# P x V in two groups per quad of heads instead of three, and two fillers at other slots

## The chip, the cores and the metric

The kernel runs on one core of a Trainium2 chip, as one program. The metric is the device time of one execution in microseconds; a kernel's time is the median of its runs. A profile is one further execution, recorded by the hardware profiler. TensorE (PE) multiplies matrices and writes PSUM; PEld is its weight load; VectorE (DVE), ScalarE (ACT) and GpSimd (POOL) do the rest; SyncE (SP) issues most DMAs.

## What is computed

One decoder layer in float32 over 16 sequences of 512 tokens with 256 features: causal attention with 16 heads of 16 features, and a feed-forward part whose hidden layer (1024) passes through butterfly stages before and after a Gelu. Cut to what matters:

```
q = x@wq + x@Aq@Bq*4;  k = x@wk;  v = x@wv + x@Av@Bv*4        # heads of 16
q, k = rope(q), rope(k)
scores = q@k.T / sqrt(16);  scores = where(causal, -1e9, scores)
out = softmax(scores) @ v                                     # "P x V"
x = layernorm(x + out@wo)
h = butterfly_up(x@W_exp + b_exp);  h = gelu(h + up_bias)
x = layernorm(x + butterfly_down(h)@W_con + b_con + down_bias)
```

The butterflies are folded into the two matrices once, at the kernel's beginning, so each sequence has a dense product into 1024 hidden units and one back.

## The kernel before, in words

A sequence is a batch `b`. Its 16 heads are worked through in four *quads* of four heads. The scores of a quad are made twice: once as queries by keys, from which VectorE takes the largest of each row (`largest`, L407), and three quads later, with these largest values put into the operands, as keys by queries, which ScalarE turns into exponentials (`weights`, L453) and which then multiply V (`weigh`, L504). Only the lower triangle is made, in four column blocks of a quad: block 0 has 512 columns, block 1 has 384, block 2 has 256, block 3 has 128.

The whole order is written out by hand. The main loop (L823) goes through *slots* `s`; a quad has five slots, `u` = 0 to 4, and a batch has 20. A batch's 20 slots are counted here as slots 0 to 19 of the batch whose row maxima are made in them; u=4 is at slots 4, 9, 14 and 19, and u=0 of the next quad at 5, 10, 15 and 0. In slots 15 to 319 of the run, both kinds of scores are made in each slot: `largest` for the quad of slot `s`, `weights` for the quad of slot `s - 15`. In the first 15 slots there is `largest` alone, in the last 15 (from 320) `weights` alone.

In each slot the loop does, in this order:

1. It takes two PSUM tiles, `pb` and `pa`, of two banks each; both pools have a single buffer. In slots u=0 to 3 `pb` receives the scores of `weights` and `pa` those of `largest`. In u=0 and u=1 that is block 0 of one pair of heads each, in u=2 and u=3 blocks 1 and 3 of one pair each. In u=4 it is block 2 of all four heads, so that each of `pb` and `pa` holds half of both kinds. The matmuls of the two kinds are issued in turn, two of the one and two of the other (four and four in u=4).
2. For `weights`: ScalarE's exponential from PSUM into the tile `pT` (L487) and POOL's causal mask on the diagonal (L491). For `largest`: VectorE's reduction with the mask added (L427), one per block and head.
3. P x V of those groups of blocks whose exponentials were made in an earlier slot (`weigh`, from the queue `due`). A quad's groups are `GROUPS`: group 0 is block 0, group 1 is blocks 1 and 3, group 2 is block 2. For every block and head there is one matmul into a quarter of the partitions of `po`; four heads fill its 128 partitions. A float32 matmul appears as two in the profile. When group 2 is done, ScalarE copies `po` to `oT` (L529).
4. The fillers: all other work, from the tables `others` and `holes`. The numbers in `add(s + ..., ...)` are the slots.

The tiles `pT` come from a pool with three buffers (L66), one per group; `po` has one.

Which group is put on the queue, and at which slot it is taken off (the entry has to be of an earlier slot):

```
if kinds[0][0] is weights and (u % 2 if len(kinds) == 2 and u < 4 else True):
    due.append((s, (*kinds[0][1], u // 2)))
...
while due and due[0][0] < (s if m < B * per else s - 1):
    weigh(*due.popleft()[1])
```

So with both kinds of scores group 0 is appended at u=1 and taken at u=2, group 1 appended at u=3 and taken at u=4, and group 2 appended at u=4 and taken at u=0 of the next quad.

The fillers that stand around the boundary of two quads, per batch, in the middle of the run:

| slot | u | P x V | fillers |
|---|---|---|---|
| 4 | 4 | group 1 | two hidden chunks (`hidden`, L631) |
| 5 | 0 | group 2 | two hidden chunks |
| 9 | 4 | group 1 | half a contraction (`contract`, L658), with add and statistics on VectorE |
| 10 | 0 | group 2 | half a contraction |
| 14 | 4 | group 1 | `project_v` of the third token block (L385), copied to `vaug` by ScalarE (L392) |
| 15 | 0 | group 2 | second half of the third contraction, with add and statistics |
| 19 | 4 | group 1 | two output projections (`project_out`, L561), each with add and statistics |
| 0 | 0 | group 2 | half a contraction |

`project_v(b, t)` makes V of token block `t` for batch `b`; V has two buffers, `vaugs[b % 2]`. In the first two and the last two batches of the run some of these fillers are elsewhere or missing; in the first two, tasks that fold the butterflies (`fold_tasks`) stand among them. The fillers that belong to a contraction take a bank of the pool `ps_w` (three banks) from the first half to VectorE's add behind the second.

Of the kernel before, what the change touches and what calls it, by code (L numbers as in the profile page):

```python
# [33 lines left out]
def decoder_layer(  # L34
# [19 lines left out]
    B, T, D = x.shape  # L54
# [449 lines left out]
    def weigh(b, c, par, group):  # L504
        pT = state.pop(("pT", b, c, par, group))
        if group == 0:
            state["po"] = ps_pv.tile([P, T], F32, tag="pv", name=f"po_{b}_{c}_{par}")
        po = state["po"]
        at = 0
        for k in GROUPS[group]:  # L510
            n = width(k)
            for g in range(NG):
                h = 2 * NG * c + 2 * g + par
                nc.tensor.matmul(  # L514
                    po[HG * g : HG * (g + 1), k * P : T],
                    vaugs[b % 2][:, k, h, :],
                    pT[:, g, at : at + n],
                    start=(k == 0),
                    stop=(group == 2),
                )  # L520
            at += n
        if group == 2:
            normalize_heads(b, c, par, po)
# [122 lines left out]
    def gelus(b, count=NHC):  # L646
        h = state["h", b]
        for hc in range(count):
            nc.scalar.activation(  # L649
                h[:, hc, :], h[:, hc, :], AF.Gelu, bias=hbias[:, hc : hc + 1]  # L650
            )
# [40 lines left out]
    def add(s, f, *args):  # L692
        others[s].append(lambda: f(*args))

    def start_projection(b, side, c):
        state["pr", b, side, c] = project(b, side, c)
# [16 lines left out]
    for b in range(B):  # L713
        s = b * per
        if b > 0:

            at = {1: (-16, -11, -13, -9), B - 1: (-4, 7, 7, 11)}.get(b, (-4, -3, 14, 11))
            for t in range(NT):
                add(s + at[t], project_v, b, t)
        if b + 1 < B:  # L720

            add(s - head * (b == 0), load_xT, b + 1)
            at = {0: (2, 5, 7, 10), 1: (3, 6, 8, 11)}.get(b, (7, 7, 7, 7))
            for i, (c, side) in enumerate(chains):
                holes.setdefault(s + at[i], []).append(
                    lambda b=b, side=side, c=c: start_projection(b + 1, side, c)
                )
                for step in range(3):
                    add(s + max(at[0] + 1 + 3 * i, at[i] + 1) + step, turn, b + 1, side, c, step)
                for step in range(1 + side):  # L730
                    add(s + max(at[0] + 1 + 3 * i, at[i] + 1) + 4 + step, part, b + 1, side, c, step)
        add(s + 5, load_x, b)
        add(s + 11, place_largest, b, 0)
        add(s + 21, place_largest, b, 1)
        for n in range(NQ):
            at = s + behind + PER_QUAD * n + 6 + (b + 1 == B)
            if at < end:
                add(at, turn_back, b, n // 2, n % 2)
        if b + 1 < B:
            for t in range(NT):  # L740
                add(s + (37, 37, 37, 38)[t], turn_heads, b, t)
                add(s + (38, 38, 39, 39)[t], project_out, b, t)
            add(s + 39, spread, 1, b)
            add(s + 40, offset, 1, b)
            add(s + 41, centre, 1, b)
            for c in range(NC):
                add(s + 42, turn_x1, b, c)
        if b + 2 < B:
            for hc in range(NHC):
                add(s + 43 + hc // 2, hidden, b, hc)  # L750
            holes.setdefault(s + 47, []).insert(0, lambda b=b: gelus(b))
            for t in range(NT):
                for half in range(2):
                    at = (8, 9, 10, 12, 13, 15, 20, 21)[2 * t + half]
                    add(s + 40 + at, contract, b, t, half)
            add(s + 61, spread, 2, b)
            add(s + 62, offset, 2, b)
            add(s + 62, centre, 2, b)
            add(s + 62, store, b)
# [50 lines left out]
    due = deque()  # L810

    def quad_of(s):
        n, u = divmod(s, PER_QUAD)
        return (n // NQ, n % NQ // 2, n % 2), u

    def place(blocks, ps, at=0):
        placed = []
        for block, pair in blocks:
            placed.append((block, pair, ps, at))
            at += width(block)  # L820
        return placed

    for s in range(-head, last):  # L823
        m, e = s, s - behind
        kinds = [
            (fn, *quad_of(n))
            for fn, n in ((weights, e), (largest, m))
            if 0 <= n < B * per
        ]
        parts = []  # L830
        step = 2
        if kinds and not (len(kinds) == 1 and kinds[0][2] % 2):
            u = kinds[0][2]
            pair0 = ps_b.tile([P, 2, T], F32, tag="b", name=f"pb_{s}")
            pair1 = ps_a.tile([P, 2, T], F32, tag="a", name=f"pa_{s}")
            if len(kinds) == 1:
                fn, quad, u = kinds[0]
                for r, ps in enumerate((pair0, pair1)):
                    parts.append(fn(*quad, place([(k, r) for k in GROUPS[u // 2]], ps)))
            elif u == PER_QUAD - 1:  # L840
                step = 4
                for i, (fn, quad, _) in enumerate(kinds):
                    parts.append(
                        fn(*quad, [(2, r, ps, i * 2 * P) for r, ps in enumerate((pair0, pair1))])
                    )
            else:
                for i, (fn, quad, _) in enumerate(kinds):
                    blocks = [(k, (r + i) % 2) for k, r in SLOTS[u]]
                    parts.append(fn(*quad, place(blocks, (pair0, pair1)[i])))
            if kinds[0][0] is weights and (u % 2 if len(kinds) == 2 and u < 4 else True):  # L850
                due.append((s, (*kinds[0][1], u // 2)))
        for i in range(0, max([len(p[0]) for p in parts], default=0), step):
            for p in parts:
                for f in p[0][i : i + step]:
                    f()
        for p in parts:
            p[1]()
        while due and due[0][0] < (s if m < B * per else s - 1):
            weigh(*due.popleft()[1])
        for f in others[s]:  # L860
            f()
        for f in holes.get(s, ()):
            f()
        to = 0 if s < 2 else tasks_at.get(s, len(fold))
        while given < min(to, len(fold)):
            while ahead < min(given + 3, len(fold)):
                fold[ahead][0]()
                ahead += 1
            fold[given][1]()
            given += 1  # L870
# [108 lines left out]
```

## Time and profile before

| | us |
|---|---|
| median of three runs | 1411.76 |
| lowest and highest run | 1406.98 and 1413.27 |
| the profiled execution, device time | 1415.53 |
| its span, first to last instruction | 1413.8 |
| granted TensorE clock, mean | 0.991 of full |
| TensorE matmuls | 9208 |
| bytes read from and written to HBM | 22.88 MB, 8.39 MB |

The span is what the profile's times are shares of. An engine's busy time is the time in which at least one of its instructions was under way. In a group's line, the numbers behind the bar are busy time and mean duration in ns, then the idle time of the engine just before them and what ended it. In a timeline, each line is a run of equal instructions in order of time: start, how long it lasted, engine, source line, operation, output<-inputs, shapes, and how many; a bracket at the end gives the idle time before it and the instruction that ended it. Ends of matmuls are modelled, so distances between starts are safer than durations. The batches in the middle repeat each other: in the two stretches 600.00 to 683.33 and 683.33 to 766.66 TensorE is busy for 82.84 us each, with 569 matmuls each, VectorE for 50.31 and 50.30.

### The profile page before, as it was taken

How to read it: one execution, taken by the hardware profiler on the slowest of the kernel's cores; microseconds unless marked ns; L12 is line 12 of the kernel's file. 1: busy time of each engine (PE TensorE's matmuls, PEld its weight loads, DVE VectorE, ACT ScalarE, POOL GpSimd, SP SyncE). 2: the span in 40 equal slices, each digit the busy share in tenths (PEclk: the TensorE clock that was granted, in tenths of full speed). 3: DMA queues.
4: the chain of work that ended last, by engine and by line, in shares of the span. 5: the costliest groups of instructions: out<-in, count | busy, mean ns of one | idle time of the engine just before them, and what ended most of it. 6: DMA issues, size and time to landing. Idle time of an engine off the chain costs nothing.

```text
span 1413.8 us, 24605 instructions
## 1 busy us (share of the span) xinstructions
PE 1379.7 (98%) x9208; PEld 758.6 (54%) x9208; DVE 828.0 (59%) x2846; ACT 720.1 (51%) x1120; POOL 511.0 (36%) x779
## 2 busy tenths in 40 slices
PE   8899999999999999999999999999999999998998
PEld 4454546465564645555464555545455564644565
DVE  5766656556575655657465565746556574664422
ACT  2665455544555454555445455544545555445553
POOL 3534225253342425334252433514244252521311
PEclk9998999999999999999999999999999999999999
DMA  5310000100010010001101100010011001000000
GB/s 180 114 31 16 32 31 16 61 17 32 31 47 30 17 53 24 32 31 32 46 17 42 36 32 31 23 55 16 32 46 32 31 17 60 3 31 2 16 1 30
DMA packets 36472, 50.43 MB, mean 36 GB/s; under 512 B 3704, under 2 KB 23160, under 8 KB 36352
## 3 DMA queue, kind: packets, MB, share of 16 engines
q1 hardware_dynamic: 32464, 43.30, 8.8%
q10 hardware_dynamic: 3888, 5.55, 1.3%
q8 instruction: 73, 1.20, 0.3%
q14 instruction: 47, 0.39, 0.1%
HBM read 22.88 MB, written 8.39 MB: 22 GB/s over the span
## 4 chain that ended last, share of the span: by engine, by line
PE 94%; ACT 2%; DVE 2%; issue 1%; DMA 0%; POOLq 0%; POOL 0%; DVEq 0%; ACTq 0%
PE pb L470 20%; PE py L658 17%; PE ph L631 16%; PE po L514 11%; PE pqk L339 8%; PE pwo L561 4%; PE pvv L385 4%; PE pa L418 3%; PE pto L536 2%; PE pb L418 2%; DVE junk L427 1%; PE ptm L443 1%; PE pt L614 1%; PE ptc L552 1%; PE pd L269 1%; PE pa L470 1%
## 5 line engine op out<-in xcount | busy, mean ns | idle before, releaser
L427 DVE CUSTOM_DVE_ANT_0 junk<-pa,causal 128x384 bf16<-128x384 f32 (+2 forms) x878 | 439.3, 500 | 240.9 <-PE pa L418 209.5
L487 ACT ACTIVATE pT<-pb 128x1024 f32<-128x1024 f32 (+1 forms) x314 | 293.7, 935 | 365.4 <-PE pa L418 266.6
L491 POOL TENSOR_SCALAR_AFFINE_SELECT pT<-pT 128x256 f32<-128x256 f32 x512 | 202.5, 408 | 755.6 <-ACT pT L487 751.3
L470 PE MATMUL pb<-qz,kz 17*128 17x512 f32 (+2 forms) x1756 | 330.0, 475 | 10.7 <-ACT pT L487 9.9
L418 PE MATMUL pa<-kz,qz 32*128 32x384 f32 (+3 forms) x1756 | 324.6, 469 | 3.8 <-DVE mx L427 3.7
L658 PE MATMUL py<-wdn,h 128*128 128x256 f32 x1024 | 253.3, 392 | 1.4 <-ACT h L649 1.4
L631 PE MATMUL ph<-x1T,yb 128*128 128x512 f32 x512 | 236.1, 605 | 0.0
L470 PEld LDWEIGHTS pb<-qz,kz 17*128 17x128 f32 (+1 forms) x1756 | 142.3, 184 | 154.7 <-issue 92.7
L658 PEld LDWEIGHTS py<-wdn,h 128*128 128x128 f32 x1024 | 185.2, 190 | 69.6 <-issue 43.7
L514 PE MATMUL po<-pT,vaug 128*32 128x512 f32 (+3 forms) x2048 | 179.7, 446 | 0.0
L418 PEld LDWEIGHTS pa<-kz,qz 32*128 32x128 f32 (+1 forms) x1756 | 148.7, 185 | 18.5 <-DVE mx L427 9.9
L631 PEld LDWEIGHTS ph<-x1T,yb 128*128 128x128 f32 x512 | 92.4, 190 | 115.3 <-issue 101.7
L427 DVE CUSTOM_DVE_ANT_0 junk<-pb,causal 128x256 bf16<-128x256 f32 (+3 forms) x146 | 63.6, 435 | 111.2 <-ACT pT L487 102.2
L339 PE MATMUL pqk<-xT,wqk 128*128 128x512 f32 x256 | 119.4, 617 | 0.0
L644 ACT COPY h<-ph 128x512 f32<-128x512 f32 x57 | 33.4, 585 | 147.2 <-PE ph L631 147.2
L514 PEld LDWEIGHTS po<-pT,vaug 128*32 128x32 f32 x2048 | 47.4, 109 | 103.2 <-issue 89.4
L427 DVE DVE_READ_ACCUMULATOR2_ANT mx<- 128x1 f32 x1024 | 84.8, 83 | 0.0
L339 PEld LDWEIGHTS pqk<-xT,wqk 128*128 128x128 f32 x256 | 48.6, 197 | 67.1 <-issue 55.2
L600 ACT ACTIVATE z<-z,norm 128x256 f32<-128x256 f32 x128 | 66.9, 590 | 27.6 <-DVE norm L593 27.6
L367 POOL TENSOR_TENSOR swap<-swap,rope_sb 128x512 f32<-128x512 f32 x62 | 79.8, 1287 | 0.0
L588 POOL TENSOR_TENSOR norm<-norm,power 128x4 f32<-128x4 f32 (+1 forms) x38 | 35.0, 922 | 113.7 <-DVE norm L587 111.7
L649 ACT ACTIVATE h<-h,hbias 128x512 f32<-128x512 f32 x115 | 72.0, 708 | 0.2
(96 smaller groups left out, 1419.4 us busy)
## 6 DMA issues: line engine op xcount, KB each, us to landing
xT<-in_xT SPq DMA_DIRECT2D x16, 512.0 KB
swap<-qz SPq DMA_DIRECT2D x64, 128.0 KB
swap<-kz SPq DMA_DIRECT2D x64, 128.0 KB
z<-in_x SPq DMA_DIRECT2D x16, 512.0 KB
out_y<-z SPq DMA_DIRECT2D x15, 512.0 KB
early<-in_wexpT ACTq DMA_DIRECT2D x1, 1028.0 KB
wdn<-in_wcon ACTq DMA_DIRECT2D x1, 1024.0 KB
qz<-mT SPq DMA_DIRECT2D x64, 8.0 KB
```

The source lines that it names most:

```text
L339: nc.tensor.matmul(pq, wqk[:, d, e : e + P], xTs[b][:, d, :], start=(d == 0), stop=(d == NC - 1))
L367: engine.tensor_tensor(swap, swap, rope_sb[:, 1, :], ALU.mult)
L418: lambda i=i, rows=rows, at=at, n=n, t=t, ps=ps: nc.tensor.matmul(ps[:, i, at : at + n], q[rows, par, t * P : n], k_[rows, par, 0:n], star ...
L427: lambda i=i, at=at, n=n, t=t, col=col, ps=ps: nc.vector.tensor_tensor_reduce(out=junk[:, 0:n], in0=ps[:, i, at : at + n], in1=causal[:, T ...
L470: lambda i=i, rows=rows, at=at, n=n, k=block, ps=ps: nc.tensor.matmul(ps[:, i, at : at + n], kt[rows, par, k * P : (k + 1) * P], qt[rows, ...
L487: nc.scalar.activation(pT[:, heads, 0:n], ps[:, :, at : at + n], AF.Exp)
L491: nc.gpsimd.affine_select(out=diag, in_=diag, pattern=[[0, 2], [1, P]], compare_op=ALU.is_ge, fill=0.0, base=0, channel_multiplier=-1,)
L514: nc.tensor.matmul(po[HG * g : HG * (g + 1), k * P : T], vaugs[b % 2][:, k, h, :], pT[:, g, at : at + n], start=(k == 0), stop=(group == 2),)
L600: nc.scalar.activation(zs[b][:, t, :], zs[b][:, t, :], AF.Identity, bias=norm[:, 2, t : t + 1], scale=norm[:, 1, t : t + 1],)
L631: nc.tensor.matmul(ph, wup[:, c, hc * P : (hc + 1) * P], state["x1T", b][:, c, :], start=(c == 0), stop=(c == NC - 1),)
L649: nc.scalar.activation(h[:, hc, :], h[:, hc, :], AF.Gelu, bias=hbias[:, hc : hc + 1])
L658: nc.tensor.matmul(py, state["h", b][:, hc, t * P : (t + 1) * P], wdn[:, hc, :], start=(hc == 0), stop=(hc == NHC - 1),)
```

## The change

With both kinds of scores, group 1 is entered one slot later, so that it is taken off the queue with group 2: at u=0 of the next quad, P x V runs over blocks 1 and 3 (384 and 128 columns) and then block 2 (256 columns), one after the other. Group 0 stays at u=2.

Two fillers change their slots. `project_v` of the third token block of batch `b` goes from slot 14 of its own batch to slot 15 of the batch before (`s - 5` for `s + 14`), for batches 2 to 14. The second half of the third contraction goes from slot 15 to slot 14 (`s + 54` for `s + 55`).

```
-            at = {1: (-16, -11, -13, -9), B - 1: (-4, 7, 7, 11)}.get(b, (-4, -3, 14, 11))
+            at = {1: (-16, -11, -13, -9), B - 1: (-4, 7, 7, 11)}.get(b, (-4, -3, -5, 11))
             for t in range(NT):
                 add(s + at[t], project_v, b, t)
...
-                    at = (8, 9, 10, 12, 13, 15, 20, 21)[2 * t + half]
+                    at = (8, 9, 10, 12, 13, 14, 20, 21)[2 * t + half]
                     add(s + 40 + at, contract, b, t, half)
...
             if kinds[0][0] is weights and (u % 2 if len(kinds) == 2 and u < 4 else True):
-                due.append((s, (*kinds[0][1], u // 2)))
+
+                due.append((s + (len(kinds) == 2 and u == 3), (*kinds[0][1], u // 2)))
```

The number of instructions of each kind stays the same on every engine. On VectorE the third contraction's add and statistics come ahead of the next slot's reductions; on ScalarE the copy of that V block comes some 48 instructions earlier.

## The prediction

> **What bounds the kernel now.** I read the page first: busy times and the chain that ended last.
>
> ```profile
> PE 1379.7 (98%) x9208; PEld 758.6 (54%) x9208; DVE 828.0 (59%) x2846; ACT 720.1 (51%) x1120; POOL 511.0 (36%) x779
> ...
> PE 94%; ACT 2%; DVE 2%; issue 1%; DMA 0%; POOLq 0%; POOL 0%; DVEq 0%; ACTq 0%
> ```
>
> TensorE is busy for 98% of the span and is 94% of the chain, so the time is the sum of what stands in its queue. In the page's groups the P x V matmuls (L514) have 0.0 us of idle before them. But 98% is not the whole truth: a busy TensorE need not be at its full rate. So I went to the timeline of TensorE where one quad ends and the next begins, that is from slot u=4 to slot u=0. First the boundary of slots 9 and 10 in a middle batch (columns: start us, us, engine, line, out<-in):
>
> ```profile
> 699.37 1.07 PE L514 MATMUL po<-pT,vaug 128*32 128x384 f32 x16
> 700.37 2.00 PE L658 MATMUL py<-wdn,h 128*128 128x256 f32 x8
> 702.29 0.70 PE L470 MATMUL pb<-qz,kz 32*128 32x512 f32 x2
> 702.31 0.70 PE L418 MATMUL pa<-kz,qz 16*128 16x512 f32 x2
> ...
> 703.37 0.64 PE L514 MATMUL po<-pT,vaug 128*32 128x256 f32 x8
> 703.93 2.00 PE L658 MATMUL py<-wdn,h 128*128 128x256 f32 x8
> ```
>
> I cost a step by the distance to the start of the next, since ends are modelled. P x V group 1 takes 700.37 - 699.37 = 1.00, the half contraction 1.92, the next quad's first scores 703.37 - 702.29 = 1.08, group 2 0.56. The scores for `pb` and for `pa` start 0.02 apart: their matmuls alternate and share the array.
>
> Now slots 14 and 15 of the same batch, where the work behind group 1 is shorter, and the same place in the last batch, where there is none:
>
> ```profile
> 717.70 1.07 PE L514 MATMUL po<-pT,vaug 128*32 128x384 f32 x16
> 718.70 1.13 PE L385 MATMUL pvv<-wv_sb,xT 128*128 128x256 f32 x4
> 719.76 1.13 PE L470 MATMUL pb<-qz,kz 17*128 17x512 f32 x4
> 720.46 1.13 PE L418 MATMUL pa<-kz,qz 32*128 32x512 f32 x4
> 721.52 0.64 PE L514 MATMUL po<-pT,vaug 128*32 128x256 f32 x8
> 722.09 1.99 PE L658 MATMUL py<-wdn,h 128*128 128x256 f32 x8
> ...
> 1302.52 1.07 PE L514 MATMUL po<-pT,vaug 128*32 128x384 f32 x16
> 1304.20 1.13 PE L470 MATMUL pb<-qz,kz 17*128 17x512 f32 x4 [0.61 <-ACT pT L487]
> 1305.29 1.13 PE L418 MATMUL pa<-kz,qz 32*128 32x512 f32 x4
> 1306.35 0.64 PE L514 MATMUL po<-pT,vaug 128*32 128x256 f32 x8
> ```
>
> Here `pa` comes 0.70 and 1.09 behind `pb`, and the scores take 1.76 and 2.15, though nearly no idle time is booked: TensorE runs the two halves one after the other. In both places `pa` starts at the same distance from the end of u=4's scores: 720.46 - 717.70 = 2.76, and 1305.29 - 1302.52 = 2.77. What holds it is VectorE:
>
> ```profile
> 718.37 0.42 DVE L427 CUSTOM_DVE_ANT_0 junk<-pb,causal 128x256 bf16<-128x256 f32 x1 [1.80 <-ACT pT L487]
> ...
> 719.88 0.42 DVE L427 CUSTOM_DVE_ANT_0 junk<-pa,causal 128x256 bf16<-128x256 f32 x1
> 720.23 0.08 DVE L427 DVE_READ_ACCUMULATOR2_ANT mx<- 128x1 f32 x1
> ```
>
> After u=4 each of `pa` and `pb` holds both kinds of scores. ScalarE's exponential of `pb` ends, then VectorE makes its four reductions, two over `pb` and two over `pa`, and the last ends at 720.31, 2.61 after the scores. `pa` is written again 0.15 later. So TensorE needs about 2.77 us of other work behind u=4, or the next scores fall apart.
>
> **The change part by part.** No matmul is added or removed; P x V group 1 moves from u=4 to u=0 of the next quad, ahead of group 2.
>
> *The merging.* 512 columns per head cost 1.00 and 256 cost 0.57, so 256 columns are 0.43 and 0.14 is fixed per visit. Group 1 and 2 together are 768 columns: 1.43, not 1.57. There are 61 quads with both kinds of scores (slots 15 to 319), so merging alone is worth 61 x 0.14 = 8.5 us. It takes 1.00 out of u=4 and puts 0.86 into u=0. At u=0 nothing needs it as cover: the next scores wait for one exponential and two reductions (721.63 to 723.06 in the same VectorE timeline, 1.54 behind the scores' end at 721.52, so 1.69 with the release), and 0.57 + 1.92 = 2.49 stands there already.
>
> The Trainium skill has a rule for each side here. "TensorEngine Tiling (Array Packing)", Key Properties, says that a change of tiling mode drains the array; by it alone the change would be a gain at every quad, which is the sum of 8.5 us above. The same page, PSUM Bottleneck, says that tiling makes TensorE faster but not the reading of PSUM, which can become the bound; by it taking TensorE work out of u=4 brings nothing. This trace shows both, 0.14 per visit and 2.77 for the readers.
>
> *What u=4 still has behind its scores*, per batch of 20 slots, from the tables of slots in the code; each is the sum from the end of u=4's scores to the end of the P x V (and what moved) at u=0:
>
> - Slots 9|10, contraction of 1.92 alone. Before 703.93 - 699.37 = 4.56. After: `pb` at 1.92, `pa` at 2.77, scores end 1.06 later (721.52 - 720.46, and 1306.35 - 1305.29) at 3.83, P x V 1.43: 5.26. +0.70, in batches 2 to 14: 13 x 0.70 = 9.1.
> - Slots 19|0, two output projections, 1.92. Before 656.30 - 651.73 = 4.57. There the exponential starts a little later and the last reduction ends at 654.47, 2.74 after 651.73, so `pa` at 2.89, scores end at 3.95, with P x V 5.38. +0.81, batches 2 to 15: 14 x 0.81 = 11.3.
> - Slots 4|5, two hidden chunks, 3.63 (672.00 to 675.63), enough cover. Before 677.27 - 671.00 = 6.27, after 3.63 + 1.07 + 1.43 = 6.13. -0.14, 14 times: -2.0.
> - Slots 14|15, with both fillers moved: the half contraction (1.92) comes to 14, `project_v` (718.70 to 719.76, 1.06) goes to 15. Before 724.01 - 717.70 = 6.31. After 3.83 + 1.43 + 1.06 = 6.32: nothing, 12 times. In batches 14 and 15 slot 15 is left with 1.43 alone (their `project_v` is elsewhere): 3.83 + 1.43, and the scores of slot 16 wait 1.69 - 1.43, 0.25 more: 5.51 against 6.32 (1308.84 - 1302.52). 2 x -0.81 = -1.6.
> - Six quads differ (u=4 at slots 19, 24, 29, 34, 39 with weight folding among the fillers, 309 after the Gelus). Each lies between -0.14 (all covered) and +0.86 (u=4 was waiting anyway, so nothing is saved there). I take the middle, +0.36: 2.2, ends -0.8 and 5.2.
>
> *The moved fillers* issue no DMA and nothing on POOL, so SP's and POOL's queues keep their order. The contraction's add and statistics on VectorE (1.1 us, 702.47 to 703.57 at slot 10) now stand behind the reductions of u=4: from 2.61 to about 3.7, just ahead of the scores' end at 3.83. Were they later, u=0's reductions would be late by as much, with 2.49 of cover against 1.69. `project_v`'s copy on ScalarE (0.37) comes behind slot 15's exponential with a whole slot before its reader; it writes the V buffer whose last reader stands just ahead of it in TensorE's queue. The copy of `po` (L529, 0.59) comes 0.86 later; its reader is behind the next slot's scores. All at nothing; uncovered, 12 x 0.37 = 4 us for the copies.
>
> Sum: 9.1 + 11.3 - 2.0 - 1.6 + 2.2 = +19.0 us. The profiled execution took 1415.53 (span 1413.8, 1.7 around it); with the change 1434.5. It was 3.8 above the median of the runs, so on the median: 1411.76 + 19.0 = **1431 us**.
>
> **The rivals.**
>
> *Only the merging counts* (faster). If TensorE did not need the cover, each of 61 quads gains 0.14: -8.5, 1403. One place decides, `pa` at u=0: the last reduction of u=4 would have to end by 1.92 - 0.15 = 1.77 after the scores; it ends at 2.61 to 2.74. For it: idle booked to VectorE before TensorE's `pa` is only 3.7 us in the whole run. Against it: the two places above, where the time is lost as busy time. Chance 0.08.
>
> *The halves overlap better than at 719.76* (no change). If only half of the 1.06 behind `pa` were on the path, 27 boundaries (13 + 14) lose 0.53 less: 19.0 - 14.3 = +4.7, 1416. Against it: 1.06 in both places, with `pb` 0.70 and 1.09 ahead. Chance 0.09.
>
> *The merged group does not do what it says* (slower). If the two groups still paid 0.14 each, +8.5: +27.5, 1439. For it: group 2 has a wait of its own for POOL's masks. Against it: the masks end at 719.30, long before, and blocks 1 and 3 follow each other inside group 1 at no extra cost. Chance 0.06.
>
> **How the numbers follow.** The forecast has 0.77, with its own range 1424 to 1436 from the six odd quads (-3 to +3) and runs that differ by 6 us among themselves. The range reaches to the overlap case below and the unmerged one above: 1420 to 1440. About 0.5% (7 us) is what a measurement of this kernel can tell from no change. Faster by more: 0.06, most of the first rival. Within: 0.10, the second and the rest of the first. Slower: 0.84.
>
> **What would show it.** In the changed profile, at 9|10 and 19|0 the contraction or the projections follow u=4's scores directly, `pa`'s scores start some 0.85 and 0.97 behind `pb`'s, scores take about 1.9 and 2.0, then one P x V stretch of 24 matmuls of 1.43. At 4|5 the scores still alternate. TensorE's busy time grows by nearly all of the difference and its idle time hardly. A batch gets 0.70 + 0.81 - 0.14 = 1.37 us longer than the 83.33 of now (slot u=4's scores at 633.18 and 716.50). The prediction is wrong if `pa` starts within 0.1 of `pb` at 9|10, or if the P x V stretch is near 1.57.

## The result, and the profile after

The changed kernel takes 1434.22 us (median of 6 runs, 1432.54 to 1435.72), the kernel before 1412.14 beside it (6 runs, 1406.98 to 1415.47): a ratio of 1.0157, 95% interval 1.0138 to 1.0177. It is slower by 22.1 us; 19.0 were forecast (1431 us, range 1420 to 1440). The profiled execution took 1432.54 with a span of 1430.8, at a mean granted clock of 0.991 as before.

First the page of the changed kernel: busy times, the chain that ended last, and the groups of the score matmuls and of the P x V matmuls.

```profile
PE 1396.1 (98%) x9208; PEld 769.7 (54%) x9208; DVE 824.3 (58%) x2846; ACT 723.1 (51%) x1120; POOL 510.7 (36%) x779
...
PE 94%; DVE 2%; ACT 2%; issue 1%; DMA 0%; POOLq 0%; POOL 0%; DVEq 0%; ACTq 0%
...
L470 PE MATMUL pb<-qz,kz 17*128 17x512 f32 (+2 forms) x1756 | 331.0, 476 | 10.2 <-ACT pT L487 8.0
L418 PE MATMUL pa<-kz,qz 32*128 32x384 f32 (+3 forms) x1756 | 325.4, 469 | 2.9 <-DVE mx L427 2.8
...
L514 PE MATMUL po<-pT,vaug 128*32 128x512 f32 (+3 forms) x2048 | 167.9, 445 | 0.0
```

The same three groups on the page of the kernel before:

```profile
L470 PE MATMUL pb<-qz,kz 17*128 17x512 f32 (+2 forms) x1756 | 330.0, 475 | 10.7 <-ACT pT L487 9.9
L418 PE MATMUL pa<-kz,qz 32*128 32x384 f32 (+3 forms) x1756 | 324.6, 469 | 3.8 <-DVE mx L427 3.7
...
L514 PE MATMUL po<-pT,vaug 128*32 128x512 f32 (+3 forms) x2048 | 179.7, 446 | 0.0
```

TensorE is busy for 16.4 us more than before, and the span is 17.0 longer: the loss is booked as work, not as waiting, though the matmuls are the same 9208. P x V itself became cheaper (busy 167.9, before 179.7). The score matmuls don't last longer either (on the mean 476 and 469 ns, before 475 and 469), and each of their two groups is busy as long as before, within 1 us. So the time can only lie in how the two groups overlap, and the timeline of TensorE shows where they no longer do. These are the boundaries of slots 9|10, 14|15, 19|0 and 4|5 in a middle batch:

```profile
706.47 1.99 PE L658 MATMUL py<-wdn,h 128*128 128x256 f32 x8
708.39 1.13 PE L470 MATMUL pb<-qz,kz 32*128 32x512 f32 x4
709.24 1.13 PE L418 MATMUL pa<-kz,qz 16*128 16x512 f32 x4
710.29 1.50 PE L514 MATMUL po<-pT,vaug 128*32 128x384 f32 x24
711.73 1.99 PE L658 MATMUL py<-wdn,h 128*128 128x256 f32 x8
...
727.41 1.13 PE L470 MATMUL pb<-qz,kz 17*128 17x512 f32 x4
728.25 1.13 PE L418 MATMUL pa<-kz,qz 32*128 32x512 f32 x4
729.31 1.50 PE L514 MATMUL po<-pT,vaug 128*32 128x384 f32 x24
730.74 1.13 PE L385 MATMUL pvv<-wv_sb,xT 128*128 128x256 f32 x4
...
744.77 1.13 PE L470 MATMUL pb<-qz,kz 32*128 32x512 f32 x4
745.73 1.13 PE L418 MATMUL pa<-kz,qz 16*128 16x512 f32 x4
746.78 1.50 PE L514 MATMUL po<-pT,vaug 128*32 128x384 f32 x24
...
766.54 0.70 PE L470 MATMUL pb<-qz,kz 17*128 17x512 f32 x2
766.56 0.70 PE L418 MATMUL pa<-kz,qz 32*128 32x512 f32 x2
...
767.62 1.50 PE L514 MATMUL po<-pT,vaug 128*32 128x384 f32 x24
769.05 2.41 PE L631 MATMUL ph<-x1T,yb 128*128 128x512 f32 x5
```

P x V now comes in one stretch of 24 matmuls, 711.73 - 710.29 = 1.44 long. Ahead of it, at 9|10, all four score matmuls of `pb` run (x4, not x2 by turns), and `pa` starts 0.85 behind; the scores take 710.29 - 708.39 = 1.90, where they took 1.08. At 14|15 the same 1.90, at 19|0 2.01 with `pa` 0.96 behind. Only at 4|5, where two hidden chunks (3.63) stand ahead, do the halves still start 0.02 apart and take 1.08. VectorE at 9|10 shows what `pa` waits for:

```profile
707.14 0.42 DVE L427 CUSTOM_DVE_ANT_0 junk<-pb,causal 128x256 bf16<-128x256 f32 x1 [1.79 <-ACT pT L487]
...
709.00 0.08 DVE L427 DVE_READ_ACCUMULATOR2_ANT mx<- 128x1 f32 x1
709.00 0.42 DVE L666 TENSOR_TENSOR z<-py,z 128x256 f32<-128x256 f32 x1
```

u=4's scores ended at 706.47. The last reduction ends at 709.08, 2.61 behind them, and `pa` is written at 709.24, 2.77 behind them. Both distances are those of the profile before; only the work that used to fill them has gone. In all twelve batches of the middle, `pa` comes 2.77 behind u=4's scores at 9|10 and at 14|15.

A stretch as long as one batch, by the windows of the changed kernel (busy time of TensorE, then its weight loads, VectorE, ScalarE, GpSimd, the clock):

```profile
600.96:685.64 84.68, 84.19 (x569) 46.24 (x568) 50.08 (x174) 43.16 (x64) 31.81 (x47) 1.00 0.10 33
```

From the scores of slot 7 of one batch to those of the next it is 84.68 us, before 83.32: +1.36. TensorE's busy time in such a stretch grew from 82.84 to 84.19, +1.35, at full clock.

### The profile page after: what moved, and what is told of

It is laid out like the page before. It is cut to its first block, busy times and chain, and to the rows that moved or that the text cites. A ratio compares the mean times of both kernels' runs of the same rounds, so it can differ in the third digit from the quotient of the medians.

```text
span 1430.8 us, 24605 instructions
## 1 busy us (share of the span) xinstructions
PE 1396.1 (98%) x9208; PEld 769.7 (54%) x9208; DVE 824.3 (58%) x2846; ACT 723.1 (51%) x1120; POOL 510.7 (36%) x779
## 4 chain that ended last, share of the span: by engine, by line
PE 94%; DVE 2%; ACT 2%; issue 1%; DMA 0%; POOLq 0%; POOL 0%; DVEq 0%; ACTq 0%
PE pb L470 20%; PE py L658 17%; PE ph L631 16%; PE po L514 11%; PE pqk L339 7%; PE pa L418 5%; PE pwo L561 4%; PE pvv L385 4%; PE pto L536 2%; DVE junk L427 2%; PE pb L418 1%; PE pt L614 1%; PE ptc L552 1%; PE ptm L443 1%; PE pa L470 1%
## 5 line engine op out<-in xcount | busy, mean ns | idle before, releaser
L514 PE MATMUL po<-pT,vaug 128*32 128x512 f32 (+3 forms) x2048 | 167.9, 445 | 0.0
L418 PEld LDWEIGHTS pa<-kz,qz 32*128 32x128 f32 (+1 forms) x1756 | 149.5, 185 | 34.1 <-issue 22.1
L514 PEld LDWEIGHTS po<-pT,vaug 128*32 128x32 f32 x2048 | 51.3, 110 | 83.9 <-issue 73.5
L529 ACT COPY oT<-po 128x512 f32<-128x512 f32 x64 | 37.5, 585 | 70.5 <-PE po L514 70.5
```

The lines of the kernel that those rows point to most:

```text
L418: lambda i=i, rows=rows, at=at, n=n, t=t, ps=ps: nc.tensor.matmul(ps[:, i, at : at + n], q[rows, par, t * P : n], k_[rows, par, 0:n], star ...
L514: nc.tensor.matmul(po[HG * g : HG * (g + 1), k * P : T], vaugs[b % 2][:, k, h, :], pT[:, g, at : at + n], start=(k == 0), stop=(group == 2),)
```

## The experiments

In all of them the *period* is the mean of the twelve distances from slot 7 to slot 7 in batches 2 to 14, read from the timeline of TensorE; the *tail* is what comes after slot 7 of batch 14. Before: 83.32 and 227.8. After: 84.68 and 229.6.

### e1: only the merging

```
-                due.append((s, (*kinds[0][1], u // 2)))
+                due.append((s + (len(kinds) == 2 and u == 3), (*kinds[0][1], u // 2)))
```

> Only the third edit: P x V group 1 goes to u=0, both fillers stay where they were. Cover theory (VectorE's last reduction lets pa go 2.77 us after u=4's scores, and TensorE loses what its fillers fall short of that): slot 14 keeps project_v alone (1.06), so the scores of slot 15 again end at 3.83, but slot 15 now holds 1.43 of P x V and 1.92 of contraction: 7.18 against 6.31, +0.87 in 14 batches more than the full change has there. Full change 1434.2, minus its +0.00 x 12 and -0.81 x 2, plus 14 x 0.87: about 1448 (1445 to 1451). Rival (the loss is in TensorE's own new order, scores directly followed by a contraction and P x V in one run; the two fillers do not matter): the same as the full change, 1434.

Measured: 1450.96 (1450.14 to 1455.6), ratio 1.0262 [1.0229, 1.0296]. With the fillers left where they were, slot 14 has only `project_v` behind its scores:

```profile
731.63 1.13 PE L385 MATMUL pvv<-wv_sb,xT 128*128 128x256 f32 x4
733.31 1.13 PE L470 MATMUL pb<-qz,kz 17*128 17x512 f32 x4 [0.55 <-ACT vaug L392]
734.40 1.13 PE L418 MATMUL pa<-kz,qz 32*128 32x512 f32 x4
735.46 1.50 PE L514 MATMUL po<-pT,vaug 128*32 128x384 f32 x24
```

Now `pb` is late too (0.55 idle). The bracket names ScalarE's copy, but VectorE's second reduction over `pb` ends 0.03 after it, and `pb` starts 1.68 behind u=4's scores, as it does in the last batch of the kernel before (1304.20 - 1302.52), where no such copy stands. `pa` comes 734.40 - 731.63 = 2.77 behind them, the same distance with another filler. The usual period (ten of the twelve) is 85.55, +2.23 over before (1.37 + 0.87 expected). The two moved fillers save 0.87 of the merging's cost at this place; they don't pay for it.

### e2: only the two moved fillers

```
-             at = {1: (-16, -11, -13, -9), B - 1: (-4, 7, 7, 11)}.get(b, (-4, -3, 14, 11))
+             at = {1: (-16, -11, -13, -9), B - 1: (-4, 7, 7, 11)}.get(b, (-4, -3, -5, 11))
...
-                    at = (8, 9, 10, 12, 13, 15, 20, 21)[2 * t + half]
+                    at = (8, 9, 10, 12, 13, 14, 20, 21)[2 * t + half]
```

> Only the two fillers move, P x V stays in three groups. Cover theory: slot 14 then holds 1.00 + 1.92 = 2.92, over the 2.77, so pa starts with pb again and slot 15's scores take 1.07 in place of 1.76; slot 15 holds 0.57 + 1.06 = 1.63, just under the 1.69 that u=0 needs. Slots 14 and 15: 1.00 + 1.92 + 1.07 + 0.57 + 1.06 + 0.06 = 5.68 against 6.31, -0.63 in 14 batches: -8.9 us, 1403 (1401 to 1406), faster than both kernels. Rival: fillers do not matter, 1412.

Measured: 1407.76 (1398.4 to 1416.0, 10 runs), ratio 0.9955 [0.993, 0.998]: faster than both kernels, though less than expected (1401 to 1406). At 14|15:

```profile
711.74 1.07 PE L514 MATMUL po<-pT,vaug 128*32 128x384 f32 x16
712.75 1.99 PE L658 MATMUL py<-wdn,h 128*128 128x256 f32 x8
714.67 0.70 PE L470 MATMUL pb<-qz,kz 17*128 17x512 f32 x2
714.68 0.70 PE L418 MATMUL pa<-kz,qz 32*128 32x512 f32 x2
```

With 1.01 + 1.92 = 2.93 behind u=4 the halves alternate. The period is 82.63: -0.69, which is all of the 0.70 that the kernel before loses here. So the two parts of the change pull in opposite directions. In its profile, what is missing of the expected gain lies in the tail, 230.4 (see e11).

### e4 and e5: block 2 without its reductions

Both kernels, changed and before, without VectorE's reductions over block 2: the four at each u=4, and also those of the quads in the first 15 slots, where both leave them out alike.

```
+        if placed[0][0] == 2:
+            later = []
         return mms, lambda: [f() for f in later]
```

> The full change, with VectorE's reductions over block 2 left out (row maxima of the second token block stay 0, so that softmax is taken without its shift there): 4 x 0.5 us of VectorE less at each u=4, nothing else. Cover theory: pa is free when ScalarE's second exponential ends, 1.3 us after the scores, under the 1.92 of filler, so the scores alternate at every u=0: -0.84 x 13 at 9|10, -0.96 x 14 at 19|0, -0.84 x 14 at 14|15, some -3 in the first batches: 1434 - 40 = 1394 (1389 to 1399). Rival (TensorE's own order costs the time, or ScalarE's exponential or POOL's masks set the wait): 1434, or down by a few us.

> The kernel before with the same reductions left out. Cover theory: only slots 14|15 and the first batches were short of cover, 14 x 0.70 and some 2: about 1400 (1396 to 1404). With VectorE out of the way at u=4, the full change without these reductions should be faster than this by the merging alone, 61 x 0.14 = 8.5 us (5 to 10). If merging is worth nothing by itself, the two are equal; if the new order costs TensorE time by itself, this one is faster.

Measured: e4 1390.4 (1387.84 to 1395.74), ratio 0.9832 [0.9795, 0.987]; e5 1403.41 (1401.28 to 1406.33), ratio 0.992 [0.9896, 0.9944]. The boundary 9|10 of e4 (its line numbers are 2 higher behind the edit):

```profile
689.47 0.70 PE L472 MATMUL pb<-qz,kz 32*128 32x512 f32 x2
689.48 0.70 PE L418 MATMUL pa<-kz,qz 16*128 16x512 f32 x2
...
690.54 1.50 PE L516 MATMUL po<-pT,vaug 128*32 128x384 f32 x24
```

TensorE's matmuls are untouched, yet its scores take 1.07 again at all four boundaries, and the period falls by 2.60 from that of the changed kernel, to 82.08 (0.84 + 0.96 + 0.84 = 2.64 were lost). e5 shows the same from the other side: at 14|15 it has `project_v` alone behind group 1, as the kernel before, and its scores take 1.07 and not 1.76. So it is VectorE's use of `pb` and `pa` that pulls TensorE's scores apart. With the loss gone, merging alone remains between e5 and e4: 82.63 - 82.08 = 0.55 for four quads, 0.138 each. By the medians e4 is faster than e5 by 13.0, more than the 5 to 10 expected: 12 periods give 6.6, and from slot 15 to slot 7 of batch 2, where the butterflies are folded, e4 is 2.7 shorter in the profiles (0.8 by merging). In that stretch the clock stood at half for 17.1 us in e5 and for 13.7 in e4, which may be most of the rest.

### e9: VectorE begins with `pa`

The changed kernel with the readers of u=4 in another order: ScalarE's exponential of `pb` beside VectorE's reductions over `pa`, then the other way round. The lambdas of `largest` and `weights` got an argument for the part.

```
+        if step == 4:
+            parts[0][1]((0,))
+            parts[1][1](slice(2, 4))
+            parts[0][1]((1,))
+            parts[1][1](slice(0, 2))
```

> The changed kernel, with only the order of u=4's readers turned: VectorE reduces pa first, while ScalarE takes the exponential of pb; then ScalarE takes pa and VectorE pb. The same instructions, none left out. Theory (what holds the next scores is that VectorE's four reductions begin only behind ScalarE's first exponential): at 9|10 and 14|15 the reductions begin 0.1 behind the scores and end 2.05 behind them, so the next scores wait until 2.20 and not 2.77: they lose 0.28 (now as idle time ahead of both halves, since pb is the one held) in place of 0.84, -0.56 each. At 19|0 VectorE is busy with the projections' statistics until 0.8 behind the scores, so nothing is won there. 26 boundaries x 0.56 = 14.6: about 1420 (1415 to 1425), batch period 83.56. Rival (VectorE's own amount of work sets it, or the loss is PSUM reads by ScalarE and VectorE at once): period 84.68, 1434.

Measured: 1418.1 (1414.83 to 1421.18, 10 runs), ratio 1.0025 [1.001, 1.004]; period 83.71 (83.56 expected). VectorE at 9|10, where u=4's scores end at 703.14:

```profile
703.26 0.42 DVE L427 CUSTOM_DVE_ANT_0 junk<-pa,causal 128x256 bf16<-128x256 f32 x1 [1.24 <-PE pa L418]
...
704.77 0.42 DVE L427 CUSTOM_DVE_ANT_0 junk<-pb,causal 128x256 bf16<-128x256 f32 x1
705.12 0.08 DVE L427 DVE_READ_ACCUMULATOR2_ANT mx<- 128x1 f32 x1
```

And TensorE at the same place:

```profile
703.14 1.99 PE L658 MATMUL py<-wdn,h 128*128 128x256 f32 x8
705.30 0.70 PE L470 MATMUL pb<-qz,kz 32*128 32x512 f32 x2 [0.17 <-issue]
705.45 0.70 PE L418 MATMUL pa<-kz,qz 16*128 16x512 f32 x2
```

The reductions begin 0.12 behind the scores (in the changed kernel 0.67) and end at 705.20, 2.06 behind them; the next scores start 2.16 behind them, not 2.77, and the halves share the array again. What is still lost here is booked as idle time, since it is now `pb`, the first half, that is held. With the same instructions 16 us are won back (18.7 against e10, on the same chip), and of the 1.36 that the change had cost in a batch, 0.97: most of the price came from the 0.5 us in which VectorE stood behind the first exponential. The kernel before is still 4.2 us faster. The 0.15 a batch that are missing from the expected gain are mainly `pa`, which here starts 0.13 to 0.15 behind `pb` (scores of 1.18 and 1.20, not 1.07). At 19|0, where VectorE is still at the projections' statistics when the scores end, 0.04 were won, and TensorE idles there:

```profile
741.28 0.70 PE L470 MATMUL pb<-qz,kz 32*128 32x512 f32 x2 [0.71 <-ACT pT L487]
```

### e3: merging only under cover

The moved fillers of e2; group 1 merged with group 2 only at 4|5, and group 0 with group 1 at slot 9.

```
-                due.append((s, (*kinds[0][1], u // 2)))
+                at = s
+                if len(kinds) == 2 and 40 <= s < 300:
+                    if s % 20 == 3:
+                        at = s + 1
+                    elif s % 20 == 6:
+                        at = s + 2
+                due.append((at, (*kinds[0][1], u // 2)))
```

> The two moved fillers as in e2, and P x V merged only where other work covers the scores amply: group 1 joins group 2 at slots 4|5 (two hidden chunks, 3.63, stand behind u=4), and group 0 joins group 1 at slot 9 (slot 7 still has 7.06 of projections behind its scores); batches 2 to 14. Theory (a visit saved is worth 0.14 and a cover of more than 2.77 costs nothing): the batch period falls by 2 x 0.14 = 0.28, from e2's 82.63 to 82.35, and the median by 13 x 0.28 = 3.6 against e2's 1407.8: about 1404 (1401 to 1407); the scores of slots 5 and 8 still take 1.07 to 1.08. Rival (merging is worth nothing where group 1 is only four heads of 32 columns further along the same queue): period 82.63, 1408. Rival (holding a pT buffer longer delays an exponential): period over 82.7, 1410 or more.

Measured: 1402.75 (1399.69 to 1404.93), ratio 0.992 [0.99, 0.994]. Slot 9, where the four blocks of groups 0 and 1 now come together:

```profile
686.69 1.93 PE L514 MATMUL po<-pT,vaug 128*32 128x512 f32 x24
688.55 1.99 PE L658 MATMUL py<-wdn,h 128*128 128x256 f32 x8
```

1024 columns take 1.86, and 1.00 twice when apart. The period is 82.35, as expected to the second digit: 0.97 below the kernel before, of which the fillers are 0.69 (e2) and the two merged visits 0.28. Where merging takes no cover away, it brings its whole gain.

### e10, e11 and e12: the difference of the medians, and the last batch

e10 is the changed kernel again, e12 is e3 again. e11 is e3 with groups 1 and 2 also merged at slot 14 of the last two batches and at 4|5 of the last:

```
-                if len(kinds) == 2 and 40 <= s < 300:
-                    if s % 20 == 3:
+                if len(kinds) == 2 and s >= 40:
+                    if s % 20 == 3 or s in (293, 313):
                         at = s + 1
-                    elif s % 20 == 6:
+                    elif s % 20 == 6 and s < 300:
                         at = s + 2
```

> The changed kernel once more, for its difference from the kernel before: forecast 19.0; the spans of the two profiles differed by 17.0, from slot 15 on by 19.5, the medians by 22.1. If the excess over 19.0 is scatter of the start-up and of the runs, the difference of the medians here lies anywhere between 16 and 23, and the batch period is again 84.68; if a step was undersized, 22 again with a longer period.

> e3, and the two quads whose u=4 is slot 14 of the last two batches (294 and 314) merge groups 1 and 2 as the changed kernel does, and 4|5 merges in the last batch too. In e2's and e3's profiles slot 15 of the last batch has P x V group 2 alone: TensorE idles some 0.7 and then 0.3 there, and in both the granted clock is 0.50 for the next 4 to 6 us (in e2 from 1301 to 1307, in e3 from 1293 to 1300), where 256 columns of P x V with 128 more take 1.87 in place of 1.00 and scores 2.83 in place of 1.6. In the changed kernel the same place has 1.43 of P x V, no such gap, and full clock. Theory (a gap in TensorE brings the half clock behind it): the tail from slot 7 of batch 14 falls by 2 x 0.2 (6.32 to 5.51 there against 5.7 to 6.0) + 0.14 + about 2.7 = 3.2, from 230.4 to about 227.2, no clock under 0.95 between the Gelus and the last slot, and the median falls by as much against e3 on the same chip, to about 1399.5 (1398 to 1401.5). Rival (the clock drops by itself at some time in that batch): the drop is there again, the tail 229.9, the median only 0.5 below e3's.

> e3 once more, as the measure for e11 on the same chip: 1402.8 (1400 to 1405), batch period 82.35, tail 230.4, and the clock at half speed behind slot 15 of the last batch again if the gap causes it; full clock there and a tail near 227.7 if it came by chance.

Measured: e10 1436.82 (1434.74 to 1438.58), ratio 1.0161 [1.0138, 1.0185], period 84.69. From the scores of slot 15 to the end of the span it takes 1377.8, the changed kernel's first profile 1377.7, the kernel before 1358.2: twice +19.5. What the change touches is 19.5 slower, and the first fifteen slots, which it doesn't touch, differ by more than 2 us from one execution to the next (slot 15 starts at 55.6 before, at 53.1 and 55.2 in the two profiles of the changed kernel).

e11 1400.54 (1396.27 to 1405.48), ratio 0.9909 [0.9882, 0.9936]; e12 1404.12 (1394.77 to 1404.68), ratio 0.9919 [0.9891, 0.9947]. Their ranges overlap, so e11 is not shown to be faster than e3; both are faster than both kernels. The tails of the profiles are 225.6 for e11, 226.9 for e12 and 230.4 for e3's first profile. e12 is the same kernel as e3 and shows no drop of the clock behind slot 15 of the last batch, so the drop is not there every time, and e11 without a drop doesn't show that its merging prevents it; the last section has the lines.

## Why the prediction was right

*The merging, 0.14 per quad.* 0.138, by e4 against e5, and again in e3's period. 24 matmuls in 1.43 to 1.44.

*Cover of 2.77 behind u=4.* 2.77 at 9|10, and 2.77 in e1 with another filler. At 19|0 2.89 was forecast: 745.73 less the end of u=4's scores at 742.84 is 2.89.

*What the boundaries lose.* 0.70 + 0.81 - 0.14 = 1.37 a batch forecast, 1.36 measured in the profile shown and 1.37 in e10's. 14|15 costs as much as before in a middle batch, as forecast. In the last batch it was to be 0.81 cheaper: slot 16's scores start 5.26 behind u=4's (1324.95 - 1319.69) and take 0.15 too long, 5.41 in all against 6.32, so 0.91 cheaper.

*The six odd quads,* +0.36 each, were the softest term: the middle between two ends. From slot 15 to slot 7 of batch 2, which holds five of them, the forecast makes 5 x 0.36 less one 0.14 = 1.7; the two profiles show 1.4 and 1.8. Nothing in the prediction spoke for the middle, so that it came this near is luck. In the tail, with the sixth, the forecast's terms make 0.9; the two profiles show 1.8 and 1.4, which was not taken apart.

*The fillers at nothing.* At 14|15, where the contraction is the moved one, its add begins at 728.02 and its statistics end at 729.12, just ahead of the end of `pa`'s next scores (729.31), whose reductions VectorE starts after an idle 0.30; slot 16's scores take turns again (731.80 and 731.82). Nothing came late.

*The rivals.* That only merging counts is what e4 shows once the reductions are gone, and e3 where other work covers them; in the changed kernel it doesn't hold. Halves that overlap better, and a merged group that doesn't save, are both excluded by the 1.90 and the 1.43 in the timeline.

*The size on the median.* The sum was 19.0, the part of the profile that the change touches says 19.5, the medians 22.1 and (e10) 22.9. The sum took both kernels to run at one clock, and on the median they don't. The mean granted clock was 0.9911 over 41 runs of the kernel before and 0.9884 over 10 of the changed one, and in those 41 runs a thousandth of clock goes with 1.15 us of span (a straight line through them): 2.7 x 1.15 = 3.1 us, about what is missing. At a clock of 0.990 thirteen runs of the kernel before have spans from 1412.0 to 1413.0, and the one of the changed kernel at that clock has 1432.6, about 20 more. Why its clock is lower was not settled.

## What to carry to other kernels

Ask of work that a merging moves what it was covering: here a visit saved 0.14 us, and took 1.0 us out of a stretch in which TensorE needs 2.77 us of other work until VectorE has emptied a PSUM tile with one buffer; with the same fillers, and with merging only at two places a batch where 3.6 us or more remained, the kernel took 1402.75. A TensorE that is 98% busy can still be waiting: look for row-tiled matmuls of two tiles that appear one after the other (x4, x4) and not in turn (x2, x2). Before work is put in as cover, look at the order in which two engines read the tiles that are waited for: turning it won back 16 of the 22 us here.

## What the hardware showed besides

Short stretches at half clock follow gaps in TensorE, in single executions. Slot 15 of the last batch has too little work in e3. The windows of e3 and of e12, the same kernel, around that place (the second number is TensorE's busy time, the third from the end its clock); e3:

```profile
1289.00:1293.00 4.00, 3.35 (x28) 1.17 (x20) 2.64 (x8) 2.50 (x3) 0.41 (x1) 1.00 0.00 0
1293.00:1297.00 4.00, 3.92 (x24) 1.81 (x24) 2.35 (x9) 1.05 (x2) 0.60 (x2) 0.56 0.00 0
1297.00:1301.00 4.00, 4.00 (x27) 2.36 (x24) 0.81 (x7) 1.19 (x4) 0.57 (x2) 0.59 0.02 4
```

and e12:

```profile
1294.00:1298.00 4.00, 3.40 (x27) 1.57 (x27) 2.98 (x11) 1.50 (x2) 0.41 (x1) 1.00 0.00 0
1298.00:1302.00 4.00, 3.88 (x34) 1.57 (x28) 2.54 (x8) 1.68 (x2) 0.41 (x1) 1.00 0.00 0
```

The same gap of 0.6 brought 7 us at half clock in the one and none in the other; the tails differ by 3.6. In e2 the drop was there, and 512 columns of P x V (not 256 and 128, as e11's expectation has it) took 1.87 in place of 1.00. In e1, where TensorE idles 0.55 at 14|15 in every batch, two of the twelve periods were 87.18 and 87.20 and not 85.55, each with the clock near 0.5 for some 3 us just behind that gap. In the steady batches of the other kernels the clock never fell. They have one gap of 0.46 a batch (ahead of L443), and e9 one of 0.71 as well, at 19|0 of every batch. So in the middle batches a drop came only behind gaps, but the length of a gap doesn't tell whether it comes, and what does stays open. Most of the scatter of the runs goes with the clock (a correlation of -0.94 between span and mean clock in the 41 runs of the kernel before).

The Trainium skill, "TensorE: Matmul & The Clock Gate", Part 1, says that the array falls back to half rate after an idle window of about 3.4 us, and that this window runs freely. The half rate agrees with the 0.50 here. The free-running window agrees too: in the clock record of each profile here all changes lie on one grid with a step of 3.413 us, and the two drops in e1's middle batches begin 771.41 us apart, 226 such steps, and last one step each. Where a gap falls on this grid doesn't explain by itself why it counts only at times: eight times the 0.55 of e1 lay whole in one step, and the clock fell behind two of them. The length does not agree: gaps of 0.55 and 0.60 us were enough at times.
